# x_w's product on two column tiles, step sizes from two row groups, and B turned in two blocks, in a chain of selective scans

## The chip, the cores and the metric

The kernel runs on one core of one Trainium2 chip. A core has a matrix engine (TensorE, PE in the profile, its weight loads PEld), a vector engine (VectorE, DVE), an activation engine (ScalarE, ACT), a general engine (GpSimd, POOL), and a queue engine that mainly issues transfers (SyncE, SP). Each works through its own instructions in order, and semaphores tell one engine of another's progress. Matrix products land in PSUM[...].

The metric is the device time of one execution in microseconds (us); lower is better.

## The reference

Four layers follow one another on images of 64 x 64 with 192 channels: a two-dimensional selective scan (ss2d) with 384 inner channels, a mamba layer over rows and columns, a Toeplitz layer, and a second ss2d with 192 inner channels. What the change touches is the same in three of them: for every position, a small product gives the step size and the vectors B and C of a state-space recurrence. From mamba:

```python
x_dbl = jnp.einsum('nld,ed->nle', uc, xw)
dt, Bp, Cp = jnp.split(x_dbl, [DT_RANK, DT_RANK + DS], axis=-1)
delta = jax.nn.softplus(jnp.einsum('nlr,dr->nld', dt, dtw) + dtb)
A = -jnp.exp(Alog)

def step(h, inp):
    d_t, b_t, c_t, u_t = inp
    dA = jnp.exp(d_t[:, :, None] * A)
    h = dA * h + (d_t * u_t)[:, :, None] * b_t[:, None, :]
    y = jnp.einsum('nds,ns->nd', h, c_t)
    return (h, y)
```

There are 12 numbers of rank for the step size (R), 16 states (N), so x_w gives E = 44 rows for each position. Everything is fp32.

## The kernel before

A sequence is cut into chunks of T = 512 positions; a chunk of one direction of one image is a *job*. Each of the two ss2d layers has 4 images x 4 directions x 8 chunks = 128 jobs, and mamba has as many, 384 in all. The ss2d layers run their 32 jobs an image between an input stage (projection and convolution) and an output stage (norm, gate, projection); mamba does all of that within its jobs.

A job's channels are split into groups of 64 and its 16 states into 4 sets. A *unit* is one group with one set: four states of 64 channels, laid out as 128 partitions by 2 x 512 columns. A job has 24 units where it has 384 channels (NT = 3 tiles of 128) and 12 in the second ss2d (NT = 2 tiles of 96).

For a unit, `feed` makes the scan's inputs two units ahead: eight matmuls (L324) on two column tiles write b, the product of dt*u and B, into PSUM, from `dtuT` and from diagonal matrices `diag` that ACT builds from B (L282); ACT takes the exponential of the step size for dA (L347). `scan` runs the recurrence on DVE (L357, or L364 where the state is carried from the job before), and POOL multiplies by C (L369, hc). `collect` sums over states with matmuls (L387, y). In some units, the *direct* ones, POOL makes the product with B instead (L301, bs), and PE has no b to make. b has two buffers, so b of a unit is written once the scan two before it is over.

What a job needs is prepared during the units of the job ahead of it, by `prepare`:

- `project` (L199): x_w's product over the NT tiles into one PSUM bank, 44 rows by 512 columns; ACT copies it to `xd` (L201) and sends the rows of B and C to DRAM (`bc_dram`; L209 in mamba as two transfers, L211 in ss2d as one), from where they are loaded spread over partitions.
- `turn_b` (L219): B transposed in four blocks of 128 positions, each from 16 rows, and copied to `bt` by ACT (L221), whence diag.
- `step_size(t)` (L225): for each of the NT tiles a matmul of 12 rows by 512 columns, and ACT adds the bias into `delta` (L228).
- `finish`: softplus over delta (L232), then dt*u (L233), which goes transposed into `dtuT` by `turn` (L242, L245).

All PSUM results of these steps, and mamba's own projections (in_ps, z_ps, o_ps) and the second ss2d's fold_ps, share the pool `mm` of two buffers of one bank each, under one tag: a product may start when one of the two is free.

`when` gives each step its unit, as a distance from the job's first unit: in the first ss2d project at -29, turn_b -27, step sizes -21, -19 and -17, finish -15; in the second -21, -19, -17 and -16, -14; in mamba -24, -22, -20, -18 and -17, -15, with the input projection's first tile (L730, whose in_ps ACT and DVE read for the convolution, L742 and L747) one unit ahead of the first step size. The order of an engine's instructions comes from this order, by a scheduler that moves an instruction when what it needs, or its buffer, isn't free by its own reckoning.

Of the kernel before, what the change touches and what calls it, by code (L numbers as in the profile page):

```python
# [7 lines left out]
F32 = mybir.dt.float32  # L8
AF = mybir.ActivationFunctionType
# [7 lines left out]
N = 16  # L17
R = 12
E = R + 2 * N
T = 512  # L20
# [3 lines left out]
NB = T // 128  # L24
# [12 lines left out]
class Kernel:  # L37
# [66 lines left out]
    def run_jobs(self, jobs, pools):  # L104
# [16 lines left out]
        for i in range(min(start, -EARLY), end):  # L121
# [21 lines left out]
            for step in steps.get(i, []):  # L143
                step()

    def plan(self, jobs, order, pools):


        uses, ready = {}, {}
        for k, job in enumerate(jobs):  # L150
            job["cbc"], job["bbc"], job["diag"], job["both"], job["dtu2"] = {}, {}, {}, {}, {}
            when = {name: k * len(order) + at for name, at in job["when"].items() if isinstance(at, int)}

            near = 2 if job["carry"] is not None else 5
            dtu = when["finish"] + 3 if job["carry"] is not None else when["store"] + 5
            for j, (t, p, c) in enumerate(order):
                i, g = k * len(order) + j, 2 * t + c
                direct = c in job["direct"].get(p, ())
                reads = [("c", p, i, when["project"] + 5), ("both", g, i - AHEAD, when["finish"] + near)]
                if direct:  # L160
                    reads += [("bc", p, i - EARLY, when["project"] + 5), ("dtu2", g, i - EARLY, dtu)]
                else:
                    reads.append(("diag", p, i - AHEAD, when["turn_b"] + 5))
                for name, key, at, after in reads:
                    first, _ = uses.setdefault(name, {}).get((k, key), (at, at))
                    uses[name][k, key] = first, at
                    ready[name, k] = after
        loads = []
        for name, of in uses.items():
            bufs, turn = pools["bufs"][name], sorted(of, key=of.get)  # L170
            for j, (k, key) in enumerate(turn):
                first = of[k, key][0]
                at = max(ready[name, k], first - LEAD)
                if j >= bufs:
                    at = max(at, of[turn[j - bufs]][1] + pools["behind"])
                one = lambda part=None, job=jobs[k], name=name, key=key: self.fetch(job, name, key, pools, part)
                if name == "diag":

                    at = max(ready[name, k], first - LEAD_DIAG)
                    if j >= bufs:  # L180
                        at = max(at, of[turn[j - bufs]][1] + 3)
                    loads += [(first, at + part, lambda part=part, one=one: one(part)) for part in range(NB)]
                    at += NB - 1
                else:
                    loads.append((first, at, one))
                assert at < first, (name, k, key, at, first)
        return [one[1:] for one in sorted(loads, key=lambda one: one[0])]

    def prepare(self, job, pools):

        nc = self.nc
        prep, mm = pools["prep"], pools["mm"]
        P, NT, DI, w = job["P"], job["NT"], job["DI"], job["w"]

        def project():
            u = job["u"]
            ps = mm.tile([E, T], F32, name="xd_ps", tag="mm")
            for t in range(NT):
                nc.tensor.matmul(ps, w["xw"][:, t, :], u[:, t], start=t == 0, stop=t == NT - 1)  # L199
            xd = job["xd"] = prep.tile([E, T], F32, name="xd", bufs=1)  # L200
            nc.scalar.copy(xd, ps)  # L201
            job["bc"] = self.bcd.tile([2 * N, T], F32, name="bc_dram")
            if job["carry"] is None:

                by_half = job["bc"].rearrange("(a n) l -> a (n l)", n=2).rearrange(
                    "a (h n l) -> h a n l", h=2, n=2
                )
                for h in range(2):
                    nc.scalar.dma_start(by_half[h], xd[0 : 2 * N, h * 256 : (h + 1) * 256])  # L209
            else:  # L210
                nc.scalar.dma_start(job["bc"], xd[0 : 2 * N, :])  # L211
            job["delta"] = prep.tile([P, NT, T], F32, name="delta", bufs=1)
            job["dtu"] = prep.tile([P, NT, T], F32, name="dtu", bufs=1)
            job["dtuT"] = prep.tile([128, NB, DI], F32, name="dtuT",)

        def turn_b():
            ps = mm.tile([128, NB, N], F32, name="b_ps", tag="mm")
            for k in range(NB):
                nc.tensor.transpose(ps[:, k, :], job["xd"][0:N, k * 128 : (k + 1) * 128], self.ident[:N, :N])  # L219
            bt = job["bt"] = prep.tile([128, NB, N], F32, name="bt")  # L220
            nc.scalar.copy(bt, ps)  # L221

        def step_size(t):
            dp = mm.tile([P, T], F32, name="dt_ps", tag="mm")
            nc.tensor.matmul(  # L225
                dp, w["dtw"][2 * N : E, t * P : (t + 1) * P], job["xd"][2 * N : E, :], start=True, stop=True
            )
            nc.scalar.activation(job["delta"][:, t, :], dp, AF.Identity, bias=w["dtb"][:, t : t + 1])  # L228

        def finish():  # L230
            delta = job["delta"]
            nc.scalar.activation(delta, delta, AF.Softplus)  # L232
            (nc.gpsimd if job["carry"] is None else nc.vector).tensor_mul(job["dtu"], delta, job["u"])  # L233
            if job["carry"] is not None:
                return
            job["deltas"] = self.bcd.tile([DI, T], F32, name="delta_dram")
            nc.scalar.dma_start(job["deltas"].rearrange("(t p) l -> p t l", p=P), delta)

        def turn(t):
# [249 lines left out]
    def ss2d_scan(self, pre, u_d, y_d, P, NT, ways, A, dtb):  # L489
        tc, nc, ins = self.tc, self.nc, self.i  # L490
        DI = P * NT
        bufs = dict(c=5, bc=2, diag=5, both=6, dtu2=2) if NT == 3 else dict(c=6, bc=2, diag=6, both=6, dtu2=4)
        with (
# [27 lines left out]
            for k, (col, rev) in sorted(enumerate(ways), key=lambda one: one[1]):  # L521
                w = {"dtb": dtb[:, k, :], "A": A[:, k]}

                def weights(k=k, w=w):
                    w["xw"] = self.load(pw, "xw", ins[f"{pre}x_w"][k])
                    w["dtw"] = pw.tile([E, DI], F32, name="dtw")
                    nc.sync.dma_start(w["dtw"][2 * N : E, :], ins[f"{pre}dt_w"][k])

                for c in range(NCH - 1, -1, -1) if rev else range(NCH):
                    first = not jobs or jobs[-1]["k"] != k  # L530
                    job = {"before": {}}
# [26 lines left out]
                    if rev:  # L558
# [3 lines left out]
                        P=P, NT=NT, DI=DI, k=k, w=w, rev=rev, carry=carry, first=first, add=add, y={}, fed={},  # L562
# [142 lines left out]
    def mamba_job(self, pw, pin, mm, i, begin, rev, w, x, done, both_w, c, fixed, zero):  # L705

        nc, ins = self.nc, self.i
        P, NT = 128, 3
        DI = P * NT
        pre = "L1_"  # L710
        s = slice(c * T, (c + 1) * T)
        job = {}

        def weights():
            for name in ("in_w", "conv_w", "conv_b", "A", "D", "x_w", "dt_b"):
                w[name] = self.load(pw, name, ins[pre + name][i])
            w["dtw"] = pw.tile([E, DI], F32, name="dt_w")
            nc.sync.dma_start(w["dtw"][2 * N : E, :], ins[pre + "dt_w"][i])
            w["out_w"] = self.load(pw, "out_w", both_w)
            w["xw"], w["dtb"] = w["x_w"], w["dt_b"]  # L720
            self.neg_exp(w["A"])

        def load():
# [382 lines left out]
```

## Time and profile before

| | |
|---|---|
| median of 3 runs | 31818.84 us (31812.0 to 31833.96) |
| the profiled execution, its own time | 31794.9 us |
| its span, first to last instruction | 31793.1 us |
| granted TensorE clock, mean | 0.948 |
| PE busy | 28311.3 us, 89% |
| DVE busy | 22474.8 us, 71% |
| ACT busy | 23362.1 us, 73% |
| POOL busy | 22678.0 us, 71% |
| L199 matmuls (x_w's product), all | 2048 passes, median 592 ns each by the records |
| L225 matmuls (step sizes), all | 2048 passes, median 665 to 692 ns |
| L201 copies of xd | 384, median 575 ns |
| L228 activations into delta | 1024, median 671 to 687 ns |

An fp32 matmul stands in the trace as two passes, so counts on PE are twice those of the program. Matmuls are pipelined: the time that a pass costs PE in a row of them is the distance between starts, not the duration in the records. A line of an order of time gives the start, the time to the end of the last of the merged instructions, the engine, the line, what is written from what, the shapes, the count, and in brackets the engine's idle time before it and what ended it.

### The profile page before, as it was taken

To read this page: it belongs to the slowest core of one execution; us is meant where nothing else is said; L and a number is where in the kernel's file an instruction comes from. 1 tells how busy PE (TensorE), PEld (TensorE's weight loads), DVE (VectorE), ACT (ScalarE), POOL (GpSimd) and SP (SyncE) were. 2 spreads that over 40 slices of the span, in tenths; PEclk is the share of its full clock that TensorE was granted. 3 is DMA by queue.
4 is the path that set the end of the run, shared out by engine and by line. 5 is a ranking of instruction groups with operands and counts; after the bars stand their busy time and mean duration, and the time that the engine had idled before them with its cause. 6 is when DMAs were issued, how large, how long until landed. Compare 5 with 4: busy or idle time off the path is not lost. (4 is left out here: it accounts for less than half of the span.)

```text
span 31793.1 us, 449637 instructions
## 1 busy us (share of the span) xinstructions
PE 28311.3 (89%) x162840; PEld 13772.2 (43%) x162840; DVE 22474.8 (71%) x16587; ACT 23362.1 (73%) x50239; POOL 22678.0 (71%) x9755
## 2 busy tenths in 40 slices
PE   8997998999899699999999999999588988888888
PEld 4453554454445344444444444444355343434344
DVE  7887887788788677777777777777433267676767
ACT  7885885887688488888888888888133287878788
POOL 6884885888488488888888888888000086767777
PEclk9998999999999899999999999999788999999999
DMA  3333333333333423233333333333533444444444
GB/s 101 100 97 110 99 97 107 103 98 98 109 100 97 135 93 93 93 97 98 98 98 96 95 95 95 98 98 99 132 72 72 109 129 120 128 124 125 124 124 124
DMA packets 1565670, 3326.87 MB, mean 105 GB/s; under 512 B 343781, under 2 KB 356438, under 8 KB 1546934
## 3 DMA queue, kind: packets, MB, share of 16 engines
q1 hardware_dynamic: 1403702, 3021.19, 34.7%
q10 hardware_dynamic: 159744, 276.91, 2.6%
q8 instruction: 1289, 21.12, 0.3%
q14 instruction: 935, 7.66, 0.1%
HBM read 2137.94 MB, written 656.08 MB: 88 GB/s over the span
## 5 line engine op out<-in xcount | busy, mean ns | idle before, releaser
L369 POOL TENSOR_TENSOR hc<-h,c 128x1024 f32<-128x1024 f32 x7680 | 18189.2, 2384 | 3115.9 <-DVE h L364 1317.7
L324 PE MATMUL b<-diag,dtuT 128*64 128x256 f32 x98304 | 12805.9, 391 | 800.1 <-DVE h L364 679.9
L324 PEld LDWEIGHTS b<-diag,dtuT 128*64 128x64 f32 x98304 | 7507.3, 140 | 6835.9 <-issue 3091.1
L387 PE MATMUL y<-hc,fold 128*64 128x512 f32 x30720 | 8995.0, 598 | 587.4 <-POOL hc L369 572.6
L364 DVE TENSOR_TENSOR_SCAN h<-dA,carry,b 128x512 f32<-128x512 f32 x6720 | 8195.0, 1264 | 1805.9 <-PE b L324 1134.3
L347 ACT ACTIVATE dA<-both,A 128x512 f32<-128x512 f32 (+1 forms) x12288 | 8279.8, 711 | 203.0 <-DVE h L357 182.0
L357 DVE TENSOR_TENSOR_SCAN h<-dA,b 128x1024 f32<-128x1024 f32 x2304 | 5251.7, 2284 | 2047.7 <-PE b L324 883.2
L282 ACT ACTIVATE diag<-ident,bt 128x128 f32<-128x128 f32 x20480 | 6527.3, 391 | 124.5 <-ACT b L347 86.1
L301 POOL TENSOR_TENSOR bs<-dtu,bc 128x1024 f32<-128x1024 f32 x1536 | 3638.4, 2369 | 1479.7 <-DMA c<-bc_dram 1087.9
L387 PEld LDWEIGHTS y<-hc,fold 128*64 128x64 f32 x30720 | 2497.6, 138 | 2981.7 <-POOL hc L369 1262.0
L441 POOL MEMSET pad<- 128x13068 f32 (+1 forms) x8 | 73.4, 9177 | 3977.5 <-DMA inw<-in_L_in_w 3004.7
L347 ACT ACTIVATE b<-both,A 128x504 f32<-128x504 f32 (+1 forms) x3072 | 2078.1, 676 | 412.7 <-DVE h L364 379.8
L357 DVE TENSOR_TENSOR_SCAN h<-b,bs 128x1024 f32<-128x1024 f32 x768 | 1754.1, 2284 | 659.6 <-ACT b L347 391.2
L367 ACT COPY carry<-h 128x2 f32<-128x2 f32 x4608 | 851.4, 185 | 1367.1 <-DVE h L364 1165.5
L364 DVE TENSOR_TENSOR_SCAN h<-b,carry,bs 128x512 f32<-128x512 f32 x1344 | 1638.0, 1259 | 105.7 <-POOL hc L369 95.3
L364 DVE TENSOR_TENSOR_SCAN h<-dA,b 128x512 f32<-128x512 f32 x960 | 1112.9, 1205 | 436.2 <-ACT dA L347 175.8
L347 ACT ACT_TABLE_LOAD x1018 | 1306.1, 1283 | 15.0 <-ACT b L335 0.3
L730 PE MATMUL in_ps<-xn,in_w 96*128 96x512 f32 x1536 | 933.4, 738 | 329.4 <-DMA xn<-m_row 177.8
L747 DVE SCALAR_TENSOR_TENSOR u<-in_ps,conv_w,u 128x504 f32<-128x504 f32 (+2 forms) x1152 | 835.7, 725 | 460.3 <-ACT u L742 438.6
L233 DVE TENSOR_TENSOR dtu<-delta,u 128x1536 f32<-128x1536 f32 (+1 forms) x256 | 611.4, 2388 | 758.2 <-ACT delta L232 602.9
L242 PEld LDWEIGHTS dtu_ps<-ident,dtu 128*128 128x128 f32 (+1 forms) x4096 | 422.1, 142 | 875.7 <-issue 569.3
L730 PE MATMUL z_ps<-xn,in_w 96*128 96x512 f32 x1536 | 761.7, 618 | 0.0
(155 smaller groups left out, 22077.8 us busy)
## 6 DMA issues: line engine op xcount, KB each, us to landing
c<-bc_dram SPq DMA_DIRECT2D x3072, 256.0 KB
both<-delta SPq DMA_DIRECT2D x2048, 128.0 KB
bc<-bc_dram SPq DMA_DIRECT2D x768, 256.0 KB
both<-delta_dram SPq DMA_DIRECT2D x768, 256.0 KB
dtu<-dtu_dram SPq DMA_DIRECT2D x768, 256.0 KB
dtu<-dtu SPq DMA_DIRECT2D x1280, 128.0 KB
L_y<-out ACTq DMA_DIRECT2D x512, 256.0 KB
u<-L_u SPq DMA_DIRECT2D x160, 768.0 KB
```

The lines of the kernel that those rows point to most:

```text
L233: (nc.gpsimd if job["carry"] is None else nc.vector).tensor_mul(job["dtu"], delta, job["u"])
L282: nc.scalar.activation(to, self.ident, AF.Copy, scale=of)
L301: self.nc.gpsimd.tensor_mul(by(b), dtu, by(job["bbc"][p]))
L324: nc.tensor.matmul(to, job["dtuT"][:, k, g * 64 : (g + 1) * 64], job["diag"][p][:, k, 2 * q : 2 * q + 2, :], start=True, stop=True,)
L347: nc.scalar.activation(to[n], of, AF.Exp, scale=w["A"][:, g, 2 * p + n : 2 * p + n + 1])
L357: nc.vector.tensor_tensor_scan(h[:, way], dA[:, way], b[:, way], 0.0, ALU.mult, ALU.add)
L364: nc.vector.tensor_tensor_scan(hn[:, n, way], dA[:, n, way], by_n[:, n, way], start, ALU.mult, ALU.add)
L367: nc.scalar.copy(carry[g, p], hn[:, :, 0 if rev else T - 1])
L369: nc.gpsimd.tensor_mul(hc, h, job["cbc"][p])
L387: nc.tensor.matmul(y[c * 64 : (c + 1) * 64, :], self.fold, of, start=first == 0 and n == 0, stop=last == LAST and n == 1)
L730: nc.tensor.matmul(ps, w["in_w"][:, k, to + t * P : to + (t + 1) * P], job["xn"][:, k, :], start=k == 0, stop=k == KC - 1,)
L747: nc.vector.scalar_tensor_tensor(u[:, :, to], ps[:, :, of], tap(3 - j), u[:, :, to], ALU.mult, ALU.add)
```

## The change

x_w's weights are padded with zeros from 44 to 64 columns, and the product is made for the two halves of the chunk's 512 positions apart: one half on the array's first 64 columns, the other on the second 64, so that `xd` is 128 partitions by 256 columns, half h in partitions 64h to 64h+43. The step sizes come from the two halves: two matmuls of 256 columns, from partitions 32 to 43 and 96 to 107, into two PSUM tiles, with two activations into delta. dt_w is loaded at both places. B is transposed in two blocks of 128 x 128, of which the copy to bt takes the 16 columns of each half. bc_dram is written in two transfers in all layers.

```diff
+    def load_steps(self, pool, w, x_w, dt_w):
+
+        nc, (P, NT, _) = self.nc, x_w.shape
+        w["xw"] = pool.tile([P, NT, 64], F32, name="xw")
+        nc.gpsimd.memset(w["xw"][:, :, E:64], 0.0)
+        nc.sync.dma_start(w["xw"][:, :, 0:E], x_w)
+        w["dtw"] = pool.tile([128, dt_w.shape[1]], F32, name="dtw")
+        for h in range(2):
+            nc.sync.dma_start(w["dtw"][h * 64 + 2 * N : h * 64 + E, :], dt_w)
...
         def project():
             u = job["u"]
-            ps = mm.tile([E, T], F32, name="xd_ps", tag="mm")
+
+            ps = mm.tile([128, 256], F32, name="xd_ps", tag="mm")
             for t in range(NT):
-                nc.tensor.matmul(ps, w["xw"][:, t, :], u[:, t], start=t == 0, stop=t == NT - 1)
-            xd = job["xd"] = prep.tile([E, T], F32, name="xd", bufs=1)
+                for h in range(2):
+                    nc.tensor.matmul(
+                        ps[h * 64 : (h + 1) * 64, :], w["xw"][:, t, :], u[:, t, h * 256 : (h + 1) * 256],
+                        start=t == 0, stop=t == NT - 1,
+                    )
+            xd = job["xd"] = prep.tile([128, 256], F32, name="xd", bufs=1)
             nc.scalar.copy(xd, ps)
...
-                for h in range(2):
-                    nc.scalar.dma_start(by_half[h], xd[0 : 2 * N, h * 256 : (h + 1) * 256])
             else:
-                nc.scalar.dma_start(job["bc"], xd[0 : 2 * N, :])
+                by_half = job["bc"].rearrange("a (h l) -> h a l", h=2)
+            for h in range(2):
+                nc.scalar.dma_start(by_half[h], xd[h * 64 : h * 64 + 2 * N, :])
...
         def turn_b():
-            ps = mm.tile([128, NB, N], F32, name="b_ps", tag="mm")
-            for k in range(NB):
-                nc.tensor.transpose(ps[:, k, :], job["xd"][0:N, k * 128 : (k + 1) * 128], self.ident[:N, :N])
+            ps = mm.tile([128, 2, 128], F32, name="b_ps", tag="mm")
+            for k in range(2):
+                nc.tensor.transpose(ps[:, k, :], job["xd"][:, k * 128 : (k + 1) * 128], self.ident)
             bt = job["bt"] = prep.tile([128, NB, N], F32, name="bt")
-            nc.scalar.copy(bt, ps)
+            of = ps.rearrange("p k (h e) -> p k h e", h=2)[:, :, :, 0:N]
+            nc.scalar.copy(bt.rearrange("p (h k) n -> p k h n", h=2), of)
 
         def step_size(t):
-            dp = mm.tile([P, T], F32, name="dt_ps", tag="mm")
-            nc.tensor.matmul(
-                dp, w["dtw"][2 * N : E, t * P : (t + 1) * P], job["xd"][2 * N : E, :], start=True, stop=True
-            )
-            nc.scalar.activation(job["delta"][:, t, :], dp, AF.Identity, bias=w["dtb"][:, t : t + 1])
+            parts = []
+            for h in range(2):
+                parts.append(mm.tile([P, 256], F32, name="dt_ps", tag="mm"))
+                rows = slice(h * 64 + 2 * N, h * 64 + E)
+                nc.tensor.matmul(
+                    parts[h], w["dtw"][rows, t * P : (t + 1) * P], job["xd"][rows, :], start=True, stop=True
+                )
+            for h in range(2):
+                nc.scalar.activation(
+                    job["delta"][:, t, h * 256 : (h + 1) * 256], parts[h], AF.Identity, bias=w["dtb"][:, t : t + 1]
+                )
...
```

The two places that load the weights (`weights` in `ss2d_scan` and in `mamba_job`) call `load_steps` instead of loading x_w and dt_w themselves.

More of the change, by code (lines that the diff above doesn't have):

```diff
@@ L524, in weights @@
                 def weights(k=k, w=w):
-                    w["xw"] = self.load(pw, "xw", ins[f"{pre}x_w"][k])
-                    w["dtw"] = pw.tile([E, DI], F32, name="dtw")
-                    nc.sync.dma_start(w["dtw"][2 * N : E, :], ins[f"{pre}dt_w"][k])
+                    self.load_steps(pw, w, ins[f"{pre}x_w"][k], ins[f"{pre}dt_w"][k])
                 for c in range(NCH - 1, -1, -1) if rev else range(NCH):
@@ L714, in weights @@
         def weights():
-            for name in ("in_w", "conv_w", "conv_b", "A", "D", "x_w", "dt_b"):
+            for name in ("in_w", "conv_w", "conv_b", "A", "D", "dt_b"):
                 w[name] = self.load(pw, name, ins[pre + name][i])
-            w["dtw"] = pw.tile([E, DI], F32, name="dt_w")
-            nc.sync.dma_start(w["dtw"][2 * N : E, :], ins[pre + "dt_w"][i])
+            self.load_steps(pw, w, ins[pre + "x_w"][i], ins[pre + "dt_w"][i])
             w["out_w"] = self.load(pw, "out_w", both_w)
-            w["xw"], w["dtb"] = w["x_w"], w["dt_b"]
+            w["dtb"] = w["dt_b"]
             self.neg_exp(w["A"])
```

## The prediction

> **What bounds the kernel now.** I read the shares of busy time first, then the kernel cut into stages, then who waited for whom in a stage, and last the order of time around the instructions that the change touches. Shares of the whole span decide nothing here: three stages run the changed code, and they differ.
>
> The copies of xd (L201, 384 of them, one a job) split the span: the first ss2d takes four blocks of 32 jobs, 70.6 us a job; mamba takes 128 jobs, 87.9 us each; the second ss2d takes 4 times 32 jobs, 39.2 us each. A table of stretches inside these stages:
>
> ```profile
> core 0: us, PE busy (x) PEld busy (x) DVE busy (x) ACT busy (x) POOL busy (x), PEclk, DMA share, GB/s
> 600.00:2200.00 1600.00, 1510.72 (x10185) 801.07 (x10181) 1365.10 (x1118) 1341.01 (x3295) 1403.78 (x599) 0.97 0.38 98
> 12000.00:22000.00 10000.00, 9466.04 (x50885) 4135.91 (x50882) 7181.93 (x4210) 8205.20 (x15114) 8768.51 (x3872) 0.97 0.31 97
> 25700.00:26600.00 900.00, 817.92 (x4780) 406.10 (x4781) 694.52 (x580) 837.74 (x2131) 803.22 (x335) 1.00 0.48 131
> ```
>
> In the first ss2d TensorE (PE) is busy 94% and nobody else is over 88%: PE sets the pace. In mamba PE seems as busy, but its work summed from starts (below) is some 75 of 88 us; the rest is waiting. In the second ss2d ScalarE (ACT) leads with 93%.
>
> The order of time on PE in the first ss2d, around x_w's product (L199) and a step size (L225):
>
> ```profile
> 4934.78 1.89 PE L387 MATMUL y<-hc,fold 128*64 128x512 f32 x8
> 4936.50 2.31 PE L199 MATMUL xd_ps<-u,xw 128*44 128x512 f32 x5
> 4938.22 0.65 PE L324 MATMUL b<-diag,dtuT 128*64 128x256 f32 x2
> 4938.64 0.59 PE L199 MATMUL xd_ps<-u,xw 128*44 128x512 f32 x1
> ...
> 4944.34 0.42 PE L219 MATMUL b_ps<-ident,xd 16*128 16x16 f32 x4
> 4944.68 1.95 PE L324 MATMUL b<-diag,dtuT 128*64 128x256 f32 x16
> ...
> 4958.62 1.12 PE L225 MATMUL dt_ps<-xd,dtw 12*128 12x512 f32 x2
> 4960.10 1.95 PE L324 MATMUL b<-diag,dtuT 128*64 128x256 f32 x16 [0.36 <-DVE h L364]
> ```
>
> Each fp32 matmul stands as two passes, and a pass of 512 columns takes 0.427 us of PE (1.89 us for 8 passes of y in pairs; starts 0.427 us apart). L199 is six passes one after the other on one column tile, 2.56 us; L324 and L387 run on two column tiles, and in the records the two of a pair start 7 ns apart. VectorE (DVE) in the same stretch:
>
> ```profile
> 4937.82 2.43 DVE L364 TENSOR_TENSOR_SCAN h<-b,carry,bs 128x512 f32<-128x512 f32 x2
> 4941.12 5.04 DVE L364 TENSOR_TENSOR_SCAN h<-dA,carry,b 128x512 f32<-128x512 f32 x4 [0.86 <-ACT diag L282]
> ...
> 4968.56 2.45 DVE L364 TENSOR_TENSOR_SCAN h<-dA,carry,b 128x512 f32<-128x512 f32 x2 [1.34 <-PE b L324]
> ```
>
> The scan stands still 0.86 us behind x_w's product and 1.34 us behind the third step size. The first is put down to ACT's diag, but the scan starts 0.15 us after the late b matmuls: it is PE. Followed back from the end of the stretch, the chain of waits holds 2.2 us of L199 and 2.2 us of L225 a job.
>
> Mamba hangs elsewhere: PE waits for the load of xn, right behind x_w's product:
>
> ```profile
> PE in_ps L730 <- DMA xn<-m_col: 148.4, 63, 3.5
> PE in_ps L730 <- DMA xn<-m_row: 127.1, 51, 3.9
> ```
>
> That is 275 us in 114 jobs of the stretch, 2.4 us a job, and followed back the chain has 12 us of this load a job and no L199, but 2.1 us of L225.
>
> **What the Trainium skill says.** "TensorEngine Tiling (Array Packing)", Key Properties: different tiles load weights and multiply in parallel, and a change of tiling mode drains the engine. The trace agrees on both: pairs 7 ns apart, and L225 (12 rows, a 32-row tile) costs 1.14 us from the end of y's work to the next b, where its two passes are 0.853: 0.29 us for two changes of mode. "TensorE: Matmul & The Clock Gate", Part 3 (Packing small matmuls), gives 3.07 times for four row tiles of 32; two row tiles alone are nowhere in this trace (L967's pairs, 7 ns apart, differ in rows and columns). "ScalarE: Activation LUTs", What ACT_TABLE_LOAD costs: about 0.28 us + 0.833 ns an element with a pointer bias, back-to-back ones overlapping 93 ns. L228 at 512 columns took 0.67 to 0.69 us (0.71 by the page); starts lie some 0.1 us closer than durations.
>
> **The change, part by part.**
>
> x_w's product: six matmuls of 256 columns on two column tiles replace three of 512 (NT=3): 12 passes in 6 pairs of 0.213 us, 1.28 us for 2.56. Saved 1.28 us a job, 1.32 at the granted clock 0.97 of the first ss2d; with NT=2, 0.85.
>
> Step sizes: where both halves stand together, two passes of 256 on two row tiles side by side are 0.43 for 0.853 us, with the same 0.29 of mode changes. Were row tiles not to overlap, nothing is saved; the lower end is that zero, the upper 0.43. I take 0.43, because diagonal tiles overlap. The halves need both PSUM buffers of mm, so where another product still holds one, they part. The built order shows it: in the first ss2d all three pairs stay together; in mamba the first step's second half waits for the first half's own delta (ACT), since the conv's in_ps holds the other bank until DVE has taken its taps, and stands behind three of b's eight matmuls; in the second ss2d the second half of step 0 stands where step 1 stood, and step 1's pair moves behind the next b.
>
> B's transposes: four short ones were 0.43 us with their mode changes (0.34 to the next start, 0.09 ahead). Two of 128 columns, by L242 (four in 0.43 us, plus changes 0.26 to 0.29), cost 0.50: 0.07 us more.
>
> ACT: the copy of xd is 256 columns on 128 partitions for 512 on 44; L245's copies (0.58 at 512, 0.47 at 384 columns) give 0.36, saving 0.21. A step's two activations of 256 occupy 2 x 0.36 for 0.58 us: +0.14 each. In both ss2d bc_dram goes in two DMAs: the issue (L211) is 0.32 us and ACT starts nothing behind it meanwhile: +0.32. Sum: +0.53 first ss2d, +0.21 mamba, +0.4 second ss2d. What stands behind these on ACT is dA and diag, needed two units later.
>
> Weights: 36 loads in all gain a memset on POOL and one DMA on SP, ahead of need: zero to 10 us over the kernel; I take zero.
>
> First ss2d: the 0.86 us of DVE's stall at x_w goes, and the remaining 0.4 us PE gains serves the following units, where each scan waits some 0.13 us for PE (2.58 us a unit against 2.44): 1.25 us saved. Step 0 sits where PE already waits 0.36 us for DVE: nothing. Steps 1 and 2 give 0.87 us of PE, but behind step 2 comes delta, softplus (1.28 + 1.49 us of ACT) and dtu on DVE, which already waits 1.08 us a job for ACT (23.8 us in 22 jobs); half passes, 0.4. Together 1.65 us x 128 = 211 us.
>
> Mamba: x_w's saving only lengthens the wait for xn: zero. Step 0 costs 0.29 us more (a second pair of mode changes), steps 1 and 2 save 0.86; by the chain's share of L225 (2.1 of 3.4 us) 0.35 remains, and ACT's added 0.21 plus its wait for a late second half takes 0.15: 0.2 us x 128 = 26 us.
>
> Second ss2d: x_w 0.85 us, of which the chain carries 1.4/1.7: 0.7 saved; step sizes 0.43 less 0.29 = 0.14. Against it: ACT comes to step 1's delta right behind diag and dA, and PE now makes that product one b later. From starts in 124 jobs: the sixteen b passes behind step 1 ended 6.8 us after it, ACT's delta started 4.4 us after it: ACT would stand some 2.4 us. The dA behind it had 2.2 to 3.6 us until their scans, so 0.5 us reach DVE, and 0.3 comes from ACT's extra work. Net zero; ends: -0.84 and +2.1 us a job.
>
> Sum: 211 + 26 + 0 = 237 us. From the profiled execution's own 31794.9 us (span 31793.1) that is 31558; the median of the runs shown is 24 us above the profiled one: 31582, I say 31580.
>
> **Rivals.**
>
> Fuller relief. All that the chain shows passes: 2.2 x 128 = 282 (first ss2d), 43 (mamba), 0.84 x 128 = 107: 432 us, 31390. For it: PE's 94%. Against: DVE already waits for ACT ahead of dtu.
>
> Hidden. DVE takes over in the first ss2d at 0.86 us a job (110 us), and the second loses 0.8 us a job (102 us): 31810. For it: scans of 2.44 us a unit nearly match PE's 2.58.
>
> Slower: ACT in the second ss2d. Its idle time there is 6.9%, 2.7 us a job; 2.4 of waiting and 0.4 of work use it up. It decides once ACT's lateness exceeds the 2.2 us that dA has in hand. Passing whole, less x_w's 0.7: 2.1 x 128 = 269 us lost; mamba, whose ACT also waits for halves, loses 0.5 x 128 = 64; the first ss2d gains only 115. Net +218: 32040. For it: ACT is the busiest engine there. Against: ACT stands 2 to 3.5 us a job at the fold's output, where lateness is recovered.
>
> That the change doesn't do what it says: row tiles run one after the other. That costs the first ss2d 0.4 and mamba 0.3 us a job: 31670, inside the forecast's case.
>
> **How the numbers follow.** Forecast's case 0.50 (31480 to 31700), fuller relief 0.22, hidden 0.11, slower 0.17. No change means within 0.2% (64 us, about what a measurement of this kernel can tell from none): faster 0.72, same 0.11, slower 0.17. The range 31370 to 31890 leaves out the far part of the slower case (0.12) and of the fuller relief (0.06).
>
> **What would show it.** L199's passes at 256 columns in pairs, 1.3 us a job; L225's pairs starting within some 10 ns; a job of the first ss2d at 69.0 us, of mamba 87.7, of the second 39.2; ACT waiting for dt_ps over 2 us a job in the second ss2d. It is wrong if the first ss2d gains under 0.9 us, or the second loses over 1.

## The result and the profile after

| | before | after |
|---|---|---|
| median of the runs, us | 31822.5 (4 runs) | 32178.4 (4 runs) |
| ratio, 95% interval | | 1.0112 [1.0094, 1.0129] |
| span of the profiled execution, us | 31793.1 | 32182.3 |
| a job of the first ss2d, us | 70.65 | 69.63 |
| a job of mamba, us | 87.88 | 88.74 |
| a job of the second ss2d, us | 39.18 | 42.48 |

The change made the kernel 1.1% slower, 356 us, where some 240 us were forecast as a gain. A job's time is the mean distance of two copies of xd in the profile; times 128 jobs the three differences are -131, +110 and +422 us, together 401 us, where the two spans differ by 389. So the second ss2d alone loses more than the whole kernel, mamba loses instead of standing still, and the first ss2d gains less than forecast.

PE's order of time after the change, around step sizes, x_w and the transposes of the first ss2d (start in us, length, engine, line, operation, shape):

```profile
4891.53 0.70 PE L244 MATMUL dt_ps<-xd,dtw 12*128 12x256 f32 x4
...
4942.01 1.47 PE L211 MATMUL xd_ps<-u,xw 128*64 128x256 f32 x12
4948.88 0.44 PE L234 MATMUL b_ps<-ident,xd 128*128 128x128 f32 x2
```

The products themselves do what they should: x_w takes 1.47 us for some 2.7, and a step's four passes 0.70 for 1.12. The passes of the two row groups start some 7 ns apart, so the two do work side by side. The same stretches as in the prediction, after the change:

```profile
core 0: us, PE busy (x) PEld busy (x) DVE busy (x) ACT busy (x) POOL busy (x), PEclk, DMA share, GB/s
600.00:2200.00 1600.00, 1478.41 (x10572) 813.27 (x10570) 1383.31 (x1136) 1362.29 (x3399) 1423.11 (x610) 0.96 0.38 100
12000.00:22000.00 10000.00, 9260.45 (x51430) 4178.16 (x51430) 7096.21 (x4166) 8147.34 (x15263) 8659.53 (x3831) 0.98 0.31 95
25700.00:26600.00 900.00, 784.11 (x4530) 382.19 (x4528) 672.45 (x532) 770.34 (x1988) 721.67 (x311) 0.96 0.46 122
```

In the second ss2d every engine became idler: ACT from 93 to 86%, POOL from 89 to 80%. Nobody has too much work there; they wait for one another. The waits in that stretch (engine, line, for whom; us in all, times, longest), after the change:

```profile
POOL hc L391 <- DVE h L386: 134.0, 81, 3.6
...
DVE h L386 <- ACT dA L369: 61.4, 68, 2.4
...
ACT delta L248 <- PE dt_ps L244: 46.1, 21, 4.7
ACT out L573 <- PE fold_ps L568: 38.2, 12, 3.9
```

The same waits before; of ACT's delta for dt_ps the list has none:

```profile
POOL hc L369 <- DVE h L364: 81.3, 88, 2.0
...
DVE h L364 <- ACT dA L347: 37.2, 36, 1.7
...
ACT out L553 <- PE fold_ps L548: 21.3, 12, 2.2
```

ACT now stands 2.2 us a job at a step's activation (46.1 us in 21 jobs). Here is one job, with PE, ACT, POOL and DVE in order of time:

```profile
27714.95 0.67 PE L244 MATMUL dt_ps<-xd,dtw 12*96 12x256 f32 x2
...
27718.27 0.67 PE L244 MATMUL dt_ps<-xd,dtw 12*96 12x256 f32 x2
...
27725.39 0.67 PE L244 MATMUL dt_ps<-xd,dtw 12*96 12x256 f32 x4
...
27726.10 0.47 ACT L248 ACTIVATE delta<-dt_ps,dtb 96x256 f32<-96x256 f32 x1 [1.78 <-PE dt_ps L244]
...
27733.95 2.35 POOL L391 TENSOR_TENSOR hc<-h,c 128x1024 f32<-128x1024 f32 x1 [0.16 <-POOL hc L391]
27734.29 3.09 DVE L255 TENSOR_TENSOR dtu<-delta,u 96x1024 f32<-96x1024 f32 x1 [0.56 <-ACT delta L254]
```

Step 0's halves are 3.3 us apart: in the built order a b (16 passes) and products of y stand between them, since each half has to have a bank of its own. PE stands idle at neither; ACT does, at step 1's pair, which comes 7 us later, and goes on 0.7 us after its start. Mark the last two lines as well: dtu follows late, begins 0.34 us behind POOL's hc, and takes 3.09 us. By the listing of dtu's instructions in the stretch, before and after (min/median/max in ns):

```profile
L233 DVE TENSOR_TENSOR dtu<-delta,u x22: 1196/1471/2357, 25718.1 to 26562.8; 96x1024 f32<-96x1024 f32 x22
```

```profile
L255 DVE TENSOR_TENSOR dtu<-delta,u x21: 2977/3096/3387, 25711.1 to 26586.3; 96x1024 f32<-96x1024 f32 x21
```

The same product of the same size takes twice as long. In mamba, PE's wait for xn, after:

```profile
PE in_ps L749 <- DMA xn<-m_col: 215.0, 63, 5.8
PE in_ps L749 <- DMA xn<-m_row: 186.7, 50, 6.3
```

That is 3.6 us a job where it was 2.4 (the two lines of before stand in the prediction).

### The profile page after: what moved, and what is told of

It reads as the page before. It is cut to its first block, busy times and chain, and to the rows that moved or that the text cites. A ratio compares the mean times of both kernels' runs of the same rounds, so it can differ in the third digit from the quotient of the medians.

```text
span 32182.3 us, 457498 instructions
## 1 busy us (share of the span) xinstructions
PE 28079.3 (87%) x166168; PEld 13949.1 (43%) x166168; DVE 22639.6 (70%) x16587; ACT 23437.1 (73%) x51263; POOL 22536.4 (70%) x9791
## 5 line engine op out<-in xcount | busy, mean ns | idle before, releaser
L409 PE MATMUL y<-hc,fold 128*64 128x512 f32 x30720 | 9210.0, 606 | 660.4 <-POOL hc L391 653.5
L409 PEld LDWEIGHTS y<-hc,fold 128*64 128x64 f32 x30720 | 2590.0, 139 | 3054.6 <-POOL hc L391 1471.3
L255 DVE TENSOR_TENSOR dtu<-delta,u 128x1536 f32<-128x1536 f32 (+1 forms) x256 | 769.3, 3005 | 828.7 <-ACT delta L254 828.7
L761 ACT ACTIVATE u<-in_ps,conv_w 128x512 f32<-128x512 f32 x384 | 263.0, 685 | 942.6 <-PE in_ps L749 916.7
L244 PE MATMUL dt_ps<-xd,dtw 12*128 12x256 f32 (+1 forms) x4096 | 912.1, 431 | 7.5 <-ACT bt L237 5.1
```

The lines of the kernel that those rows point to most:

```text
L244: nc.tensor.matmul(parts[h], w["dtw"][rows, t * P : (t + 1) * P], job["xd"][rows, :], start=True, stop=True)
L409: nc.tensor.matmul(y[c * 64 : (c + 1) * 64, :], self.fold, of, start=first == 0 and n == 0, stop=last == LAST and n == 1)
```

## The experiments

Three theories stood at the start. *Banks*: two PSUM banks a step tie up both buffers of mm and delay the step sizes. *ACT's work*: two activations and a second DMA issue. *Shift*: x_w's product is earlier, and moves bc_dram and the loads. Each run's profile has three stages, so that one run asks three questions. The measured times, us a job, and the ratio to the kernel before:

| run | first ss2d | mamba | second ss2d | median, us | ratio [95% interval] |
|---|---|---|---|---|---|
| e1 one bank, one activation | 70.11 | 88.61 | 39.40 | 31836.8 | 1.0000 [0.9992, 1.0009] |
| e2 one bank, two activations | 68.55 | 88.57 | 39.42 | 31643.6 | 0.9938 [0.9923, 0.9953] |
| e3 x_w alone | 69.99 | 87.04 | 39.31 | 31611.0 | 0.9929 [0.9914, 0.9943] |
| e4 all but x_w | 70.28 | 89.01 | 42.62 | 32360.2 | 1.0167 [1.0150, 1.0184] |
| e5 two banks, step 0 earlier | 69.63 | 88.44 | 41.00 | 31954.9 | 1.0055 [1.0038, 1.0071] |
| e6 e2 with the old addresses | 68.56 | 87.08 | 39.43 | 31449.9 | 0.9892 [0.9877, 0.9907] |
| e7 e1, finish later | 69.95 | 88.48 | 39.41 | 31800.7 | 1.0006 [0.9997, 1.0014] |
| e8 two banks, nobody stands | 69.68 | 88.26 | 39.02 | 31691.4 | 0.9960 [0.9945, 0.9975] |
| e9 e3, finish later | 69.42 | 86.92 | 39.30 | 31517.5 | 0.9906 [0.9892, 0.9921] |
| e10 e6, 64 bytes on | 68.51 | 87.35 | 39.41 | 31479.3 | 0.9895 [0.9879, 0.9912] |
| e11 before, behind xd shifted | 70.66 | 88.23 | 39.17 | 31847.8 | 1.0012 [1.0006, 1.0019] |
| e12 changed, repaired | 69.65 | 87.12 | 39.06 | 31528.8 | 0.9914 [0.9900, 0.9927] |
| e13 e12, dtu later | 68.13 | 86.92 | 39.04 | 31328.7 | 0.9847 [0.9834, 0.9861] |
| e14 before, all shifted | 70.67 | 88.12 | 39.18 | 31851.8 | 1.0012 [1.0003, 1.0020] |
| e15 e2, behind xd as before | 68.53 | 87.00 | 39.42 | 31485.5 | 0.9897 [0.9881, 0.9914] |

**One bank a step (e1, e2).** The halves become products over all 128 rows, with zero rows in dt_w for the other half.

```diff
-w["dtw"] = pool.tile([128, dt_w.shape[1]], F32, name="dtw")
+w["dtw"] = pool.tile([128, 2, dt_w.shape[1]], F32, name="dtw", bufs=1)
+nc.gpsimd.memset(w["dtw"], 0.0)
...
+dp = mm.tile([P, 2, 256], F32, name="dt_ps", tag="mm")
 for h in range(2):
-    parts.append(mm.tile([P, 256], F32, name="dt_ps", tag="mm"))
+    nc.tensor.matmul(dp[:, h, :], w["dtw"][:, h, t * P : (t + 1) * P], job["xd"], start=True, stop=True)
```

> The changed kernel, but a step's two halves are products over all 128 rows (dt_w padded with zero rows) into the two halves of one PSUM bank, and one activation of 512 columns adds the bias. x_w on two column tiles, B's two transposes and the two DMAs of bc_dram stay. Three theories of the loss. Banks: the halves need both PSUM buffers that all products share, so step sizes stand one b later and ACT waits for them. ACT's work: two activations and a second DMA issue are 0.4 to 0.5 us more a job on the busiest engine. Shift: x_w's product is earlier and shorter, which moves xd's copy, bc_dram and the xn wait against the rest. Banks: a job of the first ss2d 69.8 us, of mamba 88.0, of the second ss2d 38.8; 31680 us. ACT's work: most of it (the DMA issue, 0.32 us) is still there, second ss2d 41.5; 32050. Shift: nothing is won back, second ss2d 42.4, mamba 88.7; 32150.

> As the kernel with one PSUM bank a step, but with the changed kernel's two activations of 256 columns. All of ACT's added work is back, the second bank is not. Banks: second ss2d 39.2 us a job, mamba 88.1, 31740 us. ACT's work: second ss2d 42.4, as in the changed kernel; 32150. Shift: 42.4 too, and mamba 88.7.

Both have 39.4 us a job in the second ss2d: without the second bank the loss is gone, and two activations with a second DMA issue cost nothing there. ACT's work as the cause is out; banks hold for the second ss2d. But mamba stayed at 88.6 in both, against that theory. And e2 with more work beats e1 by 1.6 us in the first ss2d, which nobody had expected.

**The two parts alone (e3, e4).**

```diff
 # e3: x_w split as changed, xd laid out as before
-nc.scalar.copy(xd, ps)
+for h in range(2):
+    nc.scalar.copy(xd[:, h * 256 : (h + 1) * 256], ps[h * 64 : h * 64 + E, :])
 # e4: x_w as before, xd laid out as changed
+for h in range(2):
+    nc.scalar.copy(xd[h * 64 : (h + 1) * 64, :], ps[:, h * 256 : (h + 1) * 256])
```

> The kernel before with x_w's product alone on two column tiles; two copies of 256 columns bring both halves back into xd as it was, so step sizes, transposes and DMAs are the old ones (ACT has one copy more, some 0.15 us). Banks: first ss2d 69.8 us a job, mamba 87.9, second ss2d 38.8; 31690 us. ACT's work: nearly the same, second ss2d 39.2. Shift: this part carries the loss: mamba 88.7, second ss2d 41 to 42.5; 32050 to 32150.

> The changed kernel with x_w's product as before (three or two accumulated products of 512 columns on one column tile, here 64 wide), and two copies that lay the halves out as the change has them; step sizes in two banks, transposes and DMAs as in the changed kernel. Banks: the loss is here, first ss2d 70.4 us a job, mamba 88.5, second ss2d 42.6; 32300 us. ACT's work: the same sign, second ss2d 41.5. Shift: mamba 87.9 and second ss2d 39.5; 31850.

x_w alone wins 0.66, 0.84 and loses 0.13 us a job; the shift theory falls. All but x_w loses in mamba (+1.13) and the second ss2d (+3.44). Since mamba loses in e1, e2 and e4 and not in e3, its cause is neither banks, nor activations, nor x_w's product, but something that the new layout of xd brings.

**The order in the second ss2d (e5, e8).** Are two banks dear, or only the order that they force?

```diff
-2: dict(load=-25, project=-21, turn_b=-19, step_size=(-17, -16), finish=-14,
+2: dict(load=-25, project=-21, turn_b=-19, step_size=(-18, -16), finish=-14,  # e5
+2: dict(load=-25, project=-21, turn_b=-20, step_size=(-18, -16), finish=-14,  # e8
```

> The changed kernel with one due time changed: in the second ss2d step 0 falls due at -18 in place of -17, one unit earlier, so that on PE step 1's pair stands ahead of the next b and on ACT the two activations of step 0 stand ahead of eight diag. Everything else, two banks and row groups included, is the changed kernel's. If the loss of the second ss2d is the lateness of the steps in the order (banks only through the order that they force): a job falls from 42.5 to 39.6 us, 31810 us in all. If it is the two banks or row groups as such (products or copies that wait for a bank, mode changes): it stays at 42.0 to 42.6, 32150. First ss2d and mamba as in the changed kernel, 69.6 and 88.7, under both.

> The changed kernel with two due times of the second ss2d one unit earlier: B's transposes (-20 for -19) and step 0 (-18 for -17). In the built order both halves of step 0 then stand together on PE, step 1's pair stands ahead of the next b, and ACT comes to each activation after its product. Two banks and two row groups stay. With step 0's halves still parted a job took 41.0 us and ACT stood 2.1 us a job at a delta. If that stand is the rest of the loss: 39.5 us a job, 31770 us in all. If two banks cost by themselves (fold and dtu products that wait until both are read): 40.8 to 41.2, 31940. First ss2d 69.6, mamba 88.5 as in the changed kernel.

e5 recovers 1.5 us and lies between the two theories, so that neither was right as it stood: step 1's product is now in time, but ACT stands as long at the second half of step 0, whose halves are still parted. Its waits in the stretch from 25700 to 26600 us:

```profile
POOL hc L391 <- DVE h L386: 94.2, 84, 3.5
...
ACT delta L248 <- PE dt_ps L244: 44.3, 21, 2.2
```

e8, where the transposes come one unit earlier and both banks are free in time:

```profile
POOL hc L391 <- DVE h L386: 66.7, 62, 2.6
...
DVE h L386 <- ACT dA L369: 46.4, 43, 1.8
...
ACT out L573 <- PE fold_ps L568: 12.9, 10, 1.7
...
ACT delta L248 <- PE dt_ps L244: 0.4, 1, 0.4
```

The stand is gone and a job takes 39.02 us, 0.16 less than before the change. Two banks and two row groups are still there, so neither costs anything that shows; the order that the banks forced cost all of it. (The kernel before was not run with these due times, so the 0.16 us may be theirs.)

What else moves with the order is dtu. Its mean length in this layer's 128 jobs was 1.75 us before, 3.02 after the change, 2.42 in e5, 2.28 in e8. The Trainium skill, "SBUF — State Buffer", section "SBUF: two separate sides", says that a VectorE operation with two SBUF inputs and a GpSimd operation exclude each other for a whole instruction. The trace agrees: in the job shown above, hc ended at 27736.30 (27733.95 + 2.35), and dtu 1.08 us later, about the 1.2 us that it takes alone. But it isn't so that dtu meets an hc only since the change. One was running when dtu began in 123 of 128 jobs before and in 124 after, and dtu ended 1.08 us behind it in every one of them. What changed is how much of the hc was still to come: 0.4 us before, 2.0 after (medians), 1.1 in e5 and e8. So ACT's stand of 2.2 us and some 1.3 us of dtu's waiting for POOL make up the 3.3 us lost. That is a sum and not a proof: in e5, with a stand of 2.1 us and 0.7 us more of dtu than before, the loss is 1.8, so part was absorbed there. What e8 shows is that the stand, more than half of dtu's added time and the whole loss go together.

**The addresses (e6, e10, e15, e11, e14).** In mamba, the loads of c took 12.2 us from issue to landing in after, e1 and e4, but 11.6 in before and e3 (worked out from the issues and the semaphore events of the trace, some 900 loads each). Their bytes and order are the same; what differs is where tiles lie in SBUF, the on-chip memory beside PSUM, since xd shrank and x_w's weights grew.

```diff
 # e6 (e10: + 16)
-w["dtw"] = pool.tile([128, 2, dt_w.shape[1]], F32, name="dtw", bufs=1)
+w["dtw"] = pool.tile([128, 2, dt_w.shape[1] + 8], F32, name="dtw", bufs=1)
-xd = job["xd"] = prep.tile([128, 256], F32, name="xd", bufs=1)
+xd = job["xd"] = prep.tile([128, 384], F32, name="xd", bufs=1)[:, 0:256]
```

> The kernel with one bank and two activations a step, with two buffers made wider by columns that nobody uses, so that in the first ss2d and in mamba all tiles behind xd begin at the same SBUF addresses (in mamba 96 bytes above a multiple of 512, in place of 32) as in the kernel before and in the one with x_w's part alone. Order of instructions as before the padding. Mamba is 88.6 us a job in all four kernels with the new layout of xd and 87.0 with x_w's part alone; its loads of c took 12.2 us from issue to landing in the former, 11.6 in the latter. If the loads are slower for their addresses: mamba 87.0 to 87.3, 31440 us in all. If it is something else in the new layout (the place of bc_dram's issues on ACT, the transposes): 88.4 to 88.7, 31640. First ss2d 68.5, second 39.4 under both.

> The kernel with padded buffers, padded 64 bytes more: in mamba all tiles behind the weights begin 160 bytes above a multiple of 512 (96 in the kernel before, 32 in the changed one), in the first ss2d 32 above, in the second 320. Order of instructions unchanged. If only 32 above 512 is slow (or some low offset): mamba stays at 87.1 and c's loads at 11.6 us, and the first ss2d, now at 32 itself, may lose up to 1 us a job on its 68.5; 31450 to 31570 us. If the time rises and falls with the offset in another way, mamba lies between 86.5 and 88.6. If mamba's loads differed by chance from run to run: 87.0 or 88.6 with nothing in between.

e6 gives 87.08 us a job, as foretold for addresses, and c's loads take 11.6 us. PE's wait for xn in e2 and in e6, the same instructions on every engine:

```profile
PE in_ps L748 <- DMA xn<-m_col: 214.6, 64, 6.8
PE in_ps L748 <- DMA xn<-m_row: 175.7, 48, 5.8
```

```profile
PE in_ps L748 <- DMA xn<-m_col: 146.6, 64, 3.9
PE in_ps L748 <- DMA xn<-m_row: 116.3, 48, 4.9
```

The third address, 160 bytes above a multiple of 512, is as good as 96 (c 11.6 us, mamba 87.35), and the first ss2d at 32 loses nothing. Then came the kernel before with nothing but shifted tiles, and e2 with only the tiles behind xd put back:

```diff
 # e11
-xd = job["xd"] = prep.tile([E, T], F32, name="xd", bufs=1)
+xd = job["xd"] = prep.tile([E, T + 112], F32, name="xd", bufs=1)[:, 0:T]
 # e14
-w["dtw"] = pw.tile([E, DI], F32, name="dtw")
+w["dtw"] = pw.tile([E, DI + 56], F32, name="dtw")[:, 0:DI]
 # e15
-xd = job["xd"] = prep.tile([128, 256], F32, name="xd", bufs=1)
+xd = job["xd"] = prep.tile([128, 400], F32, name="xd", bufs=1)[:, 0:256]
```

> The kernel before, with its buffer xd made wider by 112 columns that nobody uses, and nothing else: every engine's instructions stand as before, only the tiles behind xd begin 448 bytes higher, in mamba 32 bytes above a multiple of 512 in place of 96, in the first ss2d 416 in place of 480 as in the changed kernel. If addresses alone slow mamba's loads: c from 11.6 to 12.2 us, mamba from 87.9 to 89.2 us a job, 31980 us in all. If the padding helped only together with the new layout: 87.9 and 31810. First ss2d 70.6, second 39.2 under both.

> The kernel before, with dt_w's buffer made wider by 56 columns that nobody uses, so that all tiles behind the weights, xn and u too, begin 448 bytes higher: in mamba 32 bytes above a multiple of 512 in place of 96. Instructions as before on every engine. If addresses alone make mamba's loss, and xn's are part of it: mamba 88.9 to 89.4 us a job, 31930 to 32000 us in all. If xn's and u's place is nothing: 88.2, as with the tiles behind xd alone, 31850. If the effect needs the new layout's own work: at most 88.2.

> The kernel with one bank and two activations a step, with xd made wider by 144 columns that nobody uses: the tiles behind xd (delta, both, c, bc, hc) begin where the kernel before has them, modulo 512, while xn and u stay at 32. Mamba was 88.6 us a job with all at 32 and 87.1 with all at 96. If the loads of c, both and bc carry it: 87.0 to 87.3, 31450 us in all. If xn and u carry it: 88.3 to 88.6, 31630. If both do, in between.

Addresses alone do slow the old kernel, but by 0.24 to 0.35 us a job with c at 12.0 us; the 1.3 us expected was a miss. e15 gets all of its 1.5 us back with xn and u left where they were: what matters is behind xd, where delta, both, c, bc and hc lie. e14's waits for xn:

```profile
PE in_ps L730 <- DMA xn<-m_col: 184.4, 62, 5.5
PE in_ps L730 <- DMA xn<-m_row: 155.4, 51, 4.8
```

They are 3.0 us a job, up 0.6 from 2.4. Over all kernels of this document the split is clean: c's loads took 12.0 to 12.2 us where the tiles behind xd lie at 32, and 11.5 to 11.6 where they lie at 96 or 160.

Why does this cost the old kernel so little and the new layout 1.5? Part of it is the clock of PE. The four products behind the wait (in_ps) take some 2.05 us or up to 3.8. One job of before, and one of e3, after the same wait:

```profile
15236.42 3.78 PE L730 MATMUL in_ps<-xn,in_w 96*128 96x512 f32 x4 [2.10 <-DMA xn<-m_row]
```

```profile
15179.33 1.98 PE L735 MATMUL in_ps<-xn,in_w 96*128 96x512 f32 x4 [2.12 <-DMA xn<-m_row]
```

The granted clock in these two stretches is 0.50 and 1.00. In before, groups of in_ps over 2.6 us had a mean clock of 0.52, the others 0.97. Over 2.6 us were 86 of 114 groups in before, 79 of 113 in e14, but 27 of 114 in e3, 38 of 112 in e15 and 31 of 113 in e12; then again 70 of 112 in e2 and 67 of 113 in the changed kernel. The Trainium skill, "TensorE: Matmul & The Clock Gate", Part 1, says that PE's clock halves after an idle window of some 3.4 us that runs freely. The trace agrees on the window: the clock's record changes only in steps of 3.41 us. It doesn't agree that the window must be idle: in before's mamba stretch PE was busy, by its records, 0.16 to 0.61 of the 3.41 us ahead of each of the 93 falls (median 0.42), and only 18 of the 2664 other windows at full clock were as low. So a wait of 2.4 us can be enough, if it falls well into one window. Why it was enough in three jobs of four in before and in one of four in e3, with waits of the same length (2.4 and 2.5 us), stays open.

The rest of the difference is in the wait. From e6 to e2 the distance from x_w's start to in_ps grows from 13.2 to 14.3 us, and in_ps from 2.7 to 3.0; from before to e14 the distance grows from 13.4 to 14.0 only, and in_ps, slow in most jobs already, not at all (3.3 and 3.2). Most of the added distance is that SP issues the load of xn later behind x_w's start (0.4 to 1.3 us, and 0.8 to 1.2). Why this is half as much in the old kernel isn't shown.

**The place of dtu in the first ss2d (e7, e9, e13).** In e2's built order, dtu stands one scan later on DVE than in e1, in 108 of the 124 jobs that were compared.

```diff
 # e7 on e1, e9 on e3
-step_size=(-21, -19, -17), finish=-15,
+step_size=(-21, -19, -17), finish=-14,
 # e13 on e12
+step_size=(-21, -19, -16), finish=-14,
```

> The kernel with one bank and one activation a step, in which finish (softplus and the product dtu) of the first ss2d falls due at -14 in place of -15. With two activations the first ss2d took 68.5 us a job, with one 70.1, though two are more work. If that is the order (there dtu stood one scan later on VectorE): 68.5 us here too, 31640 us in all. If the two smaller activations themselves are what helps (the first can start half a product earlier): 70.1, 31840. Mamba 88.6, second ss2d 39.4 under both.

> x_w's part alone, with finish of the first ss2d due at -14 in place of -15. In the built order dtu then stands one scan later on VectorE in 56 of 124 jobs (8 without the change), which makes two groups in one profile. So far, in the profiles of three kernels, jobs with dtu one scan later took 1.1 to 2.7 us less. If its place is what costs: the 56 jobs take 67.0 to 68.6 us for 48 scans, the others 69.7, the stage 69.0 to 69.4 a job, 31500 us in all. If those jobs were shorter for another reason: both groups within 0.4 us of each other, the stage 70.0, 31610. Mamba 87.0, second ss2d 39.3.

e7 did not ask what it should: finish came later, but dtu moved in only 8 of 124 jobs. From the start of a job's first scan to that of its 48th, those took 68.1 us, the others 69.7. In e9 it moved in 56, which took 67.7 us against 70.0 for the other 68, in one profile. That comparison flatters: the two sets stand at different places of an image, and they differed by 0.9 us in the kernel before (69.8 and 70.7), with dtu in one place throughout. Compared job by job, the 48 jobs that e9 moves took 69.4 us in e3 and 67.7 in e9, and e7's 8 took 69.7 in e1 and 68.1. So the place itself is worth 1.6 to 1.7 us a job. It is also what sets e2 apart from e1: its 108 moved jobs took 69.8 us in e1 and 68.0 in e2, and the 16 others 69.0 in both.

**Both losses repaired, and dtu moved (e12, e13).** e12 is the changed kernel with e8's due times and, as in e6, xd 384 columns wide and dt_w's buffer 8 columns wider.

> The changed kernel with its two losses taken out: the second ss2d's two due times one unit earlier (as in the run with 39.0 us a job), and the buffers padded so that mamba's tiles begin where the kernel before has them, modulo 512. If these two are the whole of the loss: first ss2d 69.6, mamba 86.9, second ss2d 39.0 us a job, 31510 us in all. If mamba's loss in the changed kernel has another part (the halves of step 0 parted around b): mamba 87.6 or more, 31600.

> The repaired changed kernel with two due times of the first ss2d one unit later (step 2 at -16, finish at -14), so that dtu stands two scans later on VectorE in all 124 jobs. If dtu's place ahead of a scan that could run took what the halved products gained: first ss2d 67.0 to 68.0 us a job, 31170 to 31300 us in all. If PE or ACT hold the stage by their own work: 69.4 or more, 31500.

e12 comes out close to what was foretold in all three stages (69.65, 87.12, 39.06): the two causes are the whole loss. e13 is the fastest kernel of the study, 1.5% below the kernel before, though 68.13 and 31328.7 us lie just outside what was expected of it. How much of the 1.5% the later dtu would bring without the change is open, since the kernel before was not run with these due times. DVE and POOL around dtu in the changed kernel:

```profile
6508.17 2.45 DVE L386 TENSOR_TENSOR_SCAN h<-dA,carry,b 128x512 f32<-128x512 f32 x2 [0.92 <-ACT delta L248]
...
6510.79 2.36 POOL L391 TENSOR_TENSOR hc<-h,c 128x1024 f32<-128x1024 f32 x1 [0.22 <-DVE h L386]
6511.60 3.17 DVE L255 TENSOR_TENSOR dtu<-delta,u 128x1536 f32<-128x1536 f32 x1 [0.98 <-ACT delta L254]
...
6515.29 4.78 DVE L386 TENSOR_TENSOR_SCAN h<-dA,carry,b 128x512 f32<-128x512 f32 x4
```

Behind 6510.6 DVE runs no scan for 4.7 us: 0.98 waiting for the softplus, dtu, and an addition. What that does to the others shows in the waits from 600 to 2200 us, the changed kernel first, then e13:

```profile
PE b L346 <- DVE h L386: 120.8, 57, 4.7
...
ACT b L369 <- DVE h L386: 37.9, 23, 2.1
...
DVE dtu L255 <- ACT delta L254: 26.5, 23, 1.5
```

```profile
PE dtu_ps L264 <- DVE dtu L255: 57.9, 23, 2.8
...
PE b L346 <- DVE h L386: 34.9, 54, 1.0
...
DVE dtu L255 <- ACT delta L254: 7.7, 11, 0.9
...
ACT b L369 <- DVE h L386: 0.4, 1, 0.4
```

PE's wait for a scan falls by 3.7 us a job ((120.8 - 34.9) / 23), of which 2.5 come back as the transposes' own wait for dtu (57.9 / 23), which stops no scan; ACT's wait for a scan (37.9 us) and most of dtu's wait for the softplus are gone. The stage gains 1.5 us a job.

## Why the prediction was wrong

**First ss2d: mechanism right, size off.** Forecast 1.65 us, measured 1.02. The halves' term, 0.4, holds: the changed kernel gains 0.36 on e3, and e4 0.37 on before. The term that failed is x_w's, "the 0.86 us of DVE's stall at x_w goes, and the remaining 0.4 us PE gains serves the following units": x_w alone gave 0.66 of these 1.25. The lines of the stretch from 600 to 2200 us, before and in e3:

```profile
DVE h L364 <- PE b L324: 120.2, 132, 1.6
...
DVE h L364 <- ACT dA L347: 17.4, 20, 1.2
```

```profile
DVE h L369 <- PE b L329: 101.7, 96, 1.6
...
DVE h L369 <- ACT dA L352: 41.2, 47, 1.3
```

DVE's wait for PE's b did fall, from 5.3 to 4.4 us a job, but its wait for ACT's dA rose from 0.8 to 1.8, and PE's wait for DVE from 3.9 to 4.4; in the changed kernel the three are 3.0, 2.3 and 5.3, and of the last 4.4 stand behind dtu. The prediction named dtu's wait for ACT and let it limit the third step alone; by e9 and e13, where a later dtu lets the stage gain, it limits what PE gains anywhere in the job.

**Mamba: two terms were missing, with opposite signs.** Forecast 0.2 us of gain, measured 0.86 of loss. "x_w's saving only lengthens the wait for xn: zero" failed: x_w alone (e3) gave 0.84 us. Not that the load came sooner: in_ps starts 13.4 us behind x_w's start in before and 13.3 in e3. It is in_ps itself that fell from 3.3 to 2.3 us (means), as it took over 2.6 us, at a low clock, in 27 of 114 jobs in place of 86. The prediction put that clock at nothing; what it gave was luck. Against it stands the second missing term. The changed kernel's tiles lie where c's loads take 0.6 us longer, and in_ps starts 14.4 us behind x_w where it is 13.4 in e12 with the tiles put back: the addresses cost 1.1 us a job by e8 and e12, 1.5 by e2 and e6. No step of the prediction looked at addresses, though the diff changes the sizes of xd and of x_w's weights. The halved steps, step 0's parted pair and ACT's extra work, together forecast as 0.2 us of gain, come out near nothing: e12 is within 0.1 us of e3. The same instructions in mamba gave 88.74, 88.44 and 88.26 us (after, e5, e8), so that differences under 0.5 us between single profiles say little there; for e11 and e14 it is the timed ratios that carry the small loss.

**Second ss2d: the step that decided the sign.** The stand was foreseen, 2.4 us, and measured, 2.2. What failed is "The dA behind it had 2.2 to 3.6 us until their scans, so 0.5 us reach DVE". A job became 3.3 us longer. The slack was counted for the next dA alone; but the softplus and dtu stand behind the same activation, and dtu, late, came near the start of POOL's hc in place of its end, and took 3.0 us for 1.75. Nor was x_w's 0.7 us there to set against it: e1, e2 and e3 all have 39.3 to 39.4, no better than before's 39.18. The slower rival had this mechanism and the right place for it; it gave 2.1 us a job where 3.3 came: it had no dtu, and it counted x_w's gain. "ACT stands 2 to 3.5 us a job at the fold's output, where lateness is recovered" was wrong too: that wait was 21.3 us in the 23 jobs of the stretch, 0.9 a job, and it grew to 38.2. The fold's product needs a bank of mm itself, which may be why; that isn't shown.

The signs named ahead were good ones: x_w's and the steps' pairs, ACT's stand over 2 us, and "the second loses over 1" all answered.

## What to carry to other kernels

When a change lets one step use two buffers of a ring, look where the second half stands in the built order and what waits behind its reader; if it waits, move the due time of whoever holds the buffer before judging the change (here 1.0112 became 0.9960 by two numbers). A lateness is not absorbed by the slack of the next consumer alone: follow it to every operation behind the same instruction, up to those that an instruction of another engine can hold up. When a tile's size changes, compare the addresses of everything behind it, and measure loads from issue to landing before looking for a cause in the order.

## What was not expected of the hardware

Loads into tiles that begin 32 bytes above a multiple of 512 were slower than at 96 or 160: c, 256 KB, 12.0 to 12.2 us against 11.6, and with unchanged instructions the kernel before lost 0.12% [0.06, 0.19] in e11 and 0.12% [0.03, 0.20] in e14. The Trainium skill, "DMA: Bandwidth & Descriptors", section "How a descriptor splits into AXI transactions", says that transfers which start off a 256-byte boundary take more transactions; but by its rule one of c's rows, 4096 bytes, makes seventeen at all three offsets, so it does not tell them apart. The effect was seen in mamba only, where c's loads take over 11 us; in the ss2d layers, where c takes 3.9 to 4.2 us, 32, 416 and 480 made no difference to the job. What about the address does it stays open, and so does which of the tiles behind xd carries it.

PE's clock fell to half behind waits of 2.4 us, in windows of 3.41 us in which PE was still busy up to 0.61 of the time.

Two activations of 256 columns started 0.37 us apart and took 0.46 each, for 0.68 of one with 512.
